# Queries of a local attention stage: two rotated products summed by accumulating transposes on TensorE or by an addition on GpSimd, with a newly planned order

## The chip, the cores and the metric

The kernel runs on one core of a Trainium2 chip. The time is the device time of one execution in microseconds (us). Three runs of the kernel before gave 1647.66, 1636.26 and 1648.2 us, with a median of 1647.66 us.

The engines are named as in the profile: PE is the matrix engine (PEld its weight loads), DVE the vector engine, ACT the scalar engine, POOL is GpSimd, SP only issues transfers.

## The reference, cut to what matters

The reference is a chain of eight blocks over 2048 tokens of 128 channels, each wrapped in a residual and a layer norm. The second block is a two-layer local attention network; it is where the change lies. Per layer, with 8 heads of 64 channels and sequences of 256 tokens:

```python
qkv = shift_token(x) @ wqkv
q, k, v = split into heads
q = l2norm(q) * qs
k = l2norm(k) * ksc
q = q * cos * scale + rotate_half(q) * sin * scale
k = k * cos / scale + rotate_half(k) * sin / scale
o = softmax(mask(8 * q @ k.T)) @ v      # a window of 64 and the window before it
x = x + o @ wo
x = x + gated_mlp(layernorm(shift_token(x)))
```

So every query is a sum of two products: the projected row times a table of cosines, and the half-swapped row times a table of sines. The third block is a Mamba network (a selective scan along the sequence). After them come a mixture of experts, two wide attention layers with their own feed-forward parts, another mixture of experts, and a last attention with a ternary linear layer.

## The kernel before, in words

The program is built in six stages: `rglru`, `local_mamba`, `moe1`, `chunked`, `moe2` and `typed`. Stage `local_mamba` holds the second and third blocks for 8 sequences of 256 tokens. Four sequences are in flight in the local network at a time, and behind them up to two Mamba sequences, so that the work of several generators is mixed (`interleave`, called at the end of `local_mamba`). In the profile the stage runs from about 47 us to about 800 us; the local attention part of it ends at about 627 us, and the last Mamba sequences go on alone.

One layer of one sequence is `local_block`. It calls `local_attention`, which calls `local_qk`, the function that is changed. `local_qk` works on tiles of 128 tokens by 512 channels (8 heads), two tiles for the queries (n = 0) and two for the keys (n = 1):

- PE projects a tile into a PSUM bank `qk` (two passes of 128x512 each in the profile, line 870, the shared `mm` helper);
- ACT squares it (L1085), DVE adds up the squares per head (L1086), giving the norms `ss`;
- DVE multiplies the PSUM tile by the cosine table into `t1` (L1090) and the half-swapped PSUM tile by the sine table into `t2` (L1092); the tables carry the learned scales;
- POOL clamps the norms (L1097), ACT takes their inverse root as exponential of a logarithm (L1098, L1099);
- POOL adds `t2` onto `t1` (L1105), for the keys it also multiplies by the inverse norm (L1107); the queries' inverse norm is applied later, in the softmax;
- PE transposes the sum in four 128x128 pieces into one PSUM bank `qkt` (L1110), and ACT copies the bank to the tile `q` or `k` (L1111).

Tiles `t1` and `t2` have three buffers each, the bank `qkt` has one, shared with the softmax's transposes (`pt`, L981). With 8 sequences, 2 layers and 2 tiles there are 32 query tiles and 32 key tiles, so 64 additions on L1105, of which half belong to the queries, and 256 transposes on L1110.

After `local_qk`: PE makes the scores `sc`, DVE takes their maximum (L1147), ACT the exponentials (L1153), POOL divides by the sums (L1158, a 128x1024 tile), PE transposes (L981) and multiplies by the values. The Mamba part's heaviest work is on DVE: for each of 8 groups of states a sequence has one product (L1304), one scan (L1306) and one product (L1307) on 128x1024 elements, all called `hs`.

The order of the instructions on each engine is not that of the program text. Class `_Order` takes all instructions with their dependences and runs a list scheduler over them (`plan`): an engine that comes free takes the ready instruction with the lowest rank, where the rank is the program's priority plus a hand-set offset from the table `BIAS` (one entry for each engine, tile name and stage), and changing the kind of work costs PE and ACT the offset `STAY`. Durations for this come from the table `LENGTHS` (time until the engine can issue the next, time until the result is there). `impose` then fixes that order for every engine, the transfer queues of SP, ACT and POOL among them. On the chip an engine works strictly in the imposed order, and waits when the next instruction's inputs are not there.

Of the kernel before, what the change touches and what calls it, by code (L numbers as in the profile page):

```python
# [311 lines left out]
class _Order:  # L312
# [14 lines left out]
    STAY = dict(PE=80, ACT=740)  # L327
    BIAS = {
        "ACT  1": 100, "ACT  5": 585, "ACT bt 3": 5, "ACT bt 5": -775, "ACT d 2": -425, "ACT da 2": -45, "ACT e 2": -5, "ACT e 4": 965, "ACT e 6": -20,
        "ACT got 3": 575, "ACT h 2": -200, "ACT ix 4": 15, "ACT k 2": 265, "ACT lavp 2": 210, "ACT lnrs 1": -10, "ACT lnrs 2": -160, "ACT lnsq 1": -135,  # L330
        "ACT lnsq 2": 15, "ACT ot 2": 10, "ACT ptsb 2": -595, "ACT ptsb 6": -515, "ACT q 2": 20, "ACT qsq 2": 10, "ACT r 2": -5, "ACT rg 1": 10,
        "ACT rg 2": -915, "ACT rn 2": 15, "ACT rs 4": 340, "ACT rs 6": -690, "ACT s 6": 200, "ACT sakq 2": -10, "ACT sg 3": -550, "ACT sh 5": -2525,
        "ACT spe 1": -220, "ACT spt 1": -50, "ACT st 6": 100, "ACT sz 2": 280, "ACT v 2": 885, "ACT vs 4": 320, "ACT xchunked 2": 15, "ACT xs 2": -610,
        "DVE biasfull 3": -335, "DVE biaspart 3": -20, "DVE bt 5": -5, "DVE c 1": 590, "DVE centre 0": 320, "DVE d 2": 10, "DVE decaypart 4": -600,
        "DVE e 4": 570, "DVE four 4": 100, "DVE fs 4": -70, "DVE gate 4": 340, "DVE get 2": 200, "DVE got 4": 530, "DVE identb 0": -50, "DVE k 6": 500,
        "DVE lg 2": 2240, "DVE lo 4": -265, "DVE mv 4": -660, "DVE mv 5": 100, "DVE mv 6": -485, "DVE nm 2": -3975, "DVE nm 6": 4960, "DVE nth 4": -45,
        "DVE oh 2": -725, "DVE oh 5": -10, "DVE ptsb 2": -3895, "DVE ptsb 6": 895, "DVE put 4": -395, "DVE put 5": 55, "DVE q 5": -825, "DVE q 6": -475,
        "DVE rc 2": -1225, "DVE rc 6": 10, "DVE route 2": -55, "DVE s 5": 10, "DVE sares 2": 70, "DVE sel 2": -1590, "DVE sg 3": -140, "DVE sm 4": 2720,
        "DVE spl 1": -215, "DVE ss 2": 370, "DVE st 4": 85, "DVE st 6": 1645, "DVE sum 4": 170, "DVE t 2": 440, "DVE u 2": 250, "DVE vs 4": 50,
        "DVE we 4": 1425, "DVE xc 2": 460, "DVE xla 4": -15, "DVE xlocal 2": -5, "DVE xmoe 5": -200, "DVE xmoe 6": -580, "DVE xpf 4": -370,  # L340
        "DVE xrglru 2": 120, "DVE xsa 4": 80, "DVE z 4": -1990, "PE a 2": -100, "PE acc 5": 155, "PE b 2": -35, "PE bt 3": 75, "PE bt 5": 50,
        "PE cum 2": -995, "PE cum 4": -25, "PE cum 5": -615, "PE fold 2": 2915, "PE g 2": -4155, "PE gate 2": 785, "PE kps 4": 135, "PE less 2": 295,
        "PE lg 2": 1680, "PE lg 4": 50, "PE ln 2": -10, "PE o 2": 10, "PE o 6": -10, "PE pg 5": 150, "PE ps 4": -15, "PE pt 4": -130, "PE pu 3": 220,
        "PE py 3": -200, "PE py 5": 170, "PE qk 2": 25, "PE qkt 2": -720, "PE raw 2": -8675, "PE rows 2": 400, "PE sc 2": -50, "PE sc 4": 65, "PE sc 6": 5,
        "PE v 5": 290, "PE vps 2": 4075, "PE vps 4": 25, "PE wo 2": 75, "PE wo 6": -85, "PE wout 2": -115, "PE xin 2": 1180, "PE xps 2": -2540, "PE y 2": 20,
        "PE z 2": -450, "PE zt 5": 560, "PE zt 6": 25, "POOL d 2": 130, "POOL e 6": -30, "POOL got 4": -200, "POOL h 2": 370, "POOL k 5": 400,
        "POOL k 6": 850, "POOL km 6": 1240, "POOL mean 0": 1510, "POOL places 5": -200, "POOL q 6": 20, "POOL rest 4": -65, "POOL rg 1": -800,
        "POOL rg 2": -200, "POOL rot 2": -400, "POOL s 6": -750, "POOL t 2": 550, "POOL zero 0": -655, "POOL zeros 1": 385, "SP bc 2": -970, "SP cst 3": 5,
        "SP got 3": 355, "SP got 5": 350, "SP rottable 0": 80, "SP rows 4": 210, "SP rowschunked 4": -105, "SP vec 0": -830, "SP w 0": 15, "SP w 3": 115,
        "SP wattn 2": 585, "SP wffn 2": 705, "SP wlocal 0": 1175, "SP wmoe 4": 520, "SP xs 2": -105, "SP ybuf 5": -200,  # L350
    }
    LENGTHS = {
        "ACT  LoadActFuncSet  ": (1178, 1283), "ACT d Ln 128x512 128x512": (535, 640), "ACT da Exp 128x255 128x255": (398, 503),
        "ACT e Abs 128x256 128x256": (460, 565), "ACT e Exp 128x128 128x128": (420, 525), "ACT e Exp 128x256 128x256": (461, 566),
        "ACT e Exp 128x512 128x512": (527, 632), "ACT four Exp 128x2 128x2": (100, 205), "ACT got DMACopy 128x512 128x512": (454, 3611),
        "ACT h TensorCopy 64x255 64x255": (295, 400), "ACT lnrs Exp 128x256 128x256": (315, 420), "ACT ot TensorCopy 128x512 128x512": (486, 591),
        "ACT qsq Square 128x512 128x512": (494, 599), "ACT r Relu 128x256 128x256": (460, 565), "ACT rg Exp 128x1020 128x1020": (1039, 1144),
        "ACT rg Exp 128x1024 128x1024": (998, 1103), "ACT rg Ln 128x1024 128x1024": (950, 1055), "ACT rn Exp 128x16 128x16": (110, 215),
        "ACT rn Ln 128x16 128x16": (112, 217), "ACT rs Exp 128x2 128x2": (96, 201), "ACT rs Ln 128x2 128x2": (98, 203),
        "ACT sh Silu 128x512 128x512": (492, 597), "ACT v TensorCopy 128x512 128x512": (485, 590), "ACT xc Identity 128x256 128x256": (460, 565),  # L360
        "ACT xc Silu 128x512 128x512": (526, 631), "ACT xchunked TensorCopy 128x256 128x256": (263, 368), "ACT xmoe Identity 128x256 128x256": (404, 509),
        "ACT xs TensorCopy 33x256 33x256": (257, 362), "ACT xsq Square 128x128 128x128": (297, 402), "DVE biaspart TensorCopy 96x256 96x256": (197, 282),
        "DVE decay TensorScalarPtr 128x512 128x512": (508, 593), "DVE decaypart TensorCopy 128x512 128x512": (331, 416),
        "DVE four TensorScalarPtr 128x4 128x4": (76, 160), "DVE ge TensorScalarPtr 128x256 128x256": (380, 465),
        "DVE ge TensorScalarPtr 85x256 85x256": (372, 457), "DVE got TensorScalarPtr 128x128 128x128": (258, 343),
        "DVE h TensorTensor 128x256 128x256": (312, 397), "DVE hs TensorScalarPtr 128x1024 128x1024": (2189, 2274),
        "DVE hs TensorTensor 128x1024 128x1024": (1116, 1201), "DVE mv BNStatsAggregate 128x2 128x6": (82, 167),
        "DVE nm TensorTensor 128x8 128x8": (66, 151), "DVE ptsb TensorCopy 128x512 128x512": (589, 674), "DVE rc Reciprocal 128x16 128x16": (160, 245),
        "DVE rc Reciprocal 128x4 128x4": (84, 169), "DVE rc Reciprocal 128x8 128x8": (106, 191), "DVE rg TensorScalarPtr 128x256 128x256": (577, 662),
        "DVE rg TensorTensor 128x1024 128x1024": (1109, 1194), "DVE rottable TensorScalarPtr 128x256 128x256": (261, 346),  # L370
        "DVE s TensorScalarPtr 128x128 128x128": (247, 332), "DVE s TensorTensor 128x256 128x256": (323, 408),
        "DVE sm TensorReduce 128x16 128x512": (593, 678), "DVE ss TensorReduce 128x8 128x512": (594, 679), "DVE st BNStats 128x6 128x128": (197, 282),
        "DVE sum TensorReduce 128x32 128x448": (810, 895), "DVE t TensorScalarPtr 128x256 128x256": (384, 469),
        "DVE t TensorTensor 128x512 128x512": (593, 678), "DVE vec TensorTensor 128x1 128x1": (59, 144), "DVE vec TensorTensor 85x1 85x1": (59, 144),
        "DVE vs TensorCopy 128x512 128x512": (594, 679), "DVE wlocal TensorScalarPtr 128x682 128x682": (481, 566),
        "DVE x TensorScalarPtr 128x256 128x256": (368, 453), "DVE xc TensorScalarPtr 128x254 128x254": (383, 468),
        "DVE xc TensorScalarPtr 128x255 128x255": (384, 469), "DVE xla TensorScalarPtr 128x256 128x256": (442, 527),
        "DVE xlocal TensorTensor 128x256 128x256": (311, 396), "DVE xpf TensorScalarPtr 128x256 128x256": (562, 647),
# [393 lines left out]
class _Kernel:  # L772
# [300 lines left out]
    def local_qk(self, l, h, w, rot, work, local, small, pools):  # L1073
# [6 lines left out]
        for n in range(2):  # L1080
# [20 lines left out]
            for t in range(2):  # L1101
# [4 lines left out]
                if n:  # L1106
                    nc.gpsimd.tensor_tensor(t1, t1, rn[:, 2 + t, :].unsqueeze(2).to_broadcast([P, 8, 64]), ALU.mult)  # L1107
                for c in range(4):
                    cols = slice(c * P, (c + 1) * P)
                    nc.tensor.transpose(ps[:, cols], f1[:, cols], self.ident)  # L1110
# [1300 lines left out]
```

## Time and profile before

| what | value |
|---|---|
| median of 3 runs | 1647.66 us (1636.26 to 1648.2) |
| profiled execution, its own time | 1644.68 us |
| its span | 1642.9 us |
| mean granted PE clock | 0.942 |
| busy share of the span: PE, DVE, ACT, POOL | 86%, 67%, 59%, 36% |
| L1105, additions of `t1` and `t2` on POOL | 64, median 1272 ns, 83.9 us in all |
| L1110, transposes of queries and keys on PE | 256, median 273 ns, 40.5 us in all |

The profile gives for each group of instructions how long they kept their engine busy, how long the engine stood idle just before them, and what ended that idle time. PE pipelines its work, so that instructions overlap and a matmul's duration is longer than the distance from its start to that of the next. The table by stretch (windows) sums the busy time of each engine between two times, counted from the start of the span.

### The profile page before, as it was taken

How to read it: one execution, taken by the hardware profiler on the slowest of the kernel's cores; microseconds unless marked ns; L12 is line 12 of the kernel's file. 1: busy time of each engine (PE TensorE's matmuls, PEld its weight loads, DVE VectorE, ACT ScalarE, POOL GpSimd, SP SyncE). 2: the span in 40 equal slices, each digit the busy share in tenths (PEclk: the TensorE clock that was granted, in tenths of full speed). 3: DMA queues.
4: the chain of work that ended last, by engine and by line, in shares of the span. 5: the costliest groups of instructions: out<-in, count | busy, mean ns of one | idle time of the engine just before them, and what ended most of it. 6: DMA issues, size and time to landing. Idle time of an engine off the chain costs nothing. (4 is left out here: it accounts for less than half of the span.)

```text
span 1642.9 us, 28581 instructions
## 1 busy us (share of the span) xinstructions
PE 1417.4 (86%) x10826; PEld 909.4 (55%) x10826; DVE 1102.3 (67%) x2182; ACT 968.6 (59%) x2656; POOL 587.5 (36%) x535
## 2 busy tenths in 40 slices
PE   2688998989898887777579999999998899899997
PEld 1354554545554544334366766777675576556664
DVE  5745568898989898698545557554546333279886
ACT  3777888787978869446125545455453222167775
POOL 1334544535462523101431222212212102467774
PEclk7789999989999999779789999999998899999998
DMA  5000012121212223155430000000000130000000
GB/s 199 1 1 1 1 40 65 40 60 45 65 40 65 53 52 91 52 179 189 151 119 1 8 12 11 10 5 8 32 18 24 46 121 26 26 9 8 5 8 11
DMA packets 45113, 77.97 MB, mean 47 GB/s; under 512 B 5580, under 2 KB 21988, under 8 KB 43824
## 3 DMA queue, kind: packets, MB, share of 16 engines
q1 hardware_dynamic: 39648, 70.02, 14.0%
q0 software_dynamic: 3216, 5.07, 1.1%
q8 instruction: 85, 1.39, 0.4%
q10 hardware_dynamic: 2112, 1.05, 0.2%
q14 instruction: 52, 0.43, 0.1%
HBM read 66.87 MB, written 10.76 MB: 47 GB/s over the span
## 5 line engine op out<-in xcount | busy, mean ns | idle before, releaser
L870 PE MATMUL y<-hs,ident 128*128 128x512 f32 x256 | 139.7, 659 | 35.9 <-DVE hs L1307 35.6
L1158 POOL TENSOR_TENSOR e<-e,rc 128x1024 f32<-128x1024 f32 x32 | 78.0, 2437 | 202.7 <-DVE rc L1157 194.3
L1306 DVE TENSOR_TENSOR_SCAN hs<-da,hs 128x1024 f32<-128x1024 f32 x64 | 149.1, 2331 | 0.2
L2259 ACT ACTIVATE e<-sc,nm 128x128 f32<-128x128 f32 (+1 forms) x256 | 105.2, 427 | 46.6 <-DVE nm L2254 40.3
L1153 ACT ACTIVATE e<-sc,nm,rn 128x128 f32<-128x128 f32 x256 | 114.3, 466 | 13.8 <-DVE nm L1148 13.5
L981 PE MATMUL pt<-ident,e 128*128 128x128 f32 x768 | 114.2, 278 | 9.4 <-POOL e L1158 4.9
L1302 ACT ACTIVATE da<-d,na 128x255 f32<-128x255 f32 x256 | 109.3, 504 | 17.5 <-DVE hs L1306 13.7
L1836 POOL TENSOR_TENSOR e<-e,rc 128x512 f32<-128x512 f32 x32 | 34.0, 1064 | 219.8 <-DVE rc L1835 154.2
L981 PEld LDWEIGHTS pt<-ident,e 128*128 128x128 f32 x768 | 88.5, 141 | 42.5 <-issue 16.1
L2262 POOL TENSOR_TENSOR e<-e,rc 128x1024 f32<-128x1024 f32 x48 | 90.8, 1896 | 39.1 <-DVE rc L2261 32.1
L1105 POOL TENSOR_TENSOR t<-t,t 128x512 f32<-128x512 f32 x64 | 83.9, 1316 | 58.0 <-DVE t L1092 51.6
L1811 ACT COPY kp<-kps 128x512 f32<-128x512 f32 x128 | 74.7, 583 | 49.0 <-PE kps L870 46.4
L1658 POOL DMA_INDIRECT got<-ybuf,get x48 | 45.7, 952 | 159.2 <-DMA ybuf<-ys 97.1
L870 PEld LDWEIGHTS y<-hs,ident 128*128 128x128 f32 x256 | 48.5, 205 | 82.5 <-DVE hs L1307 54.2
L1304 DVE TENSOR_TENSOR hs<-u,bc 128x1024 f32<-128x1024 f32 x64 | 84.3, 1328 | 2.9 <-POOL u L1291 2.9
L1307 DVE TENSOR_TENSOR hs<-hs,bc 128x1024 f32<-128x1024 f32 x64 | 80.6, 1260 | 0.0
L1847 ACT COPY vs<-vps 128x512 f32<-128x512 f32 x64 | 37.4, 585 | 67.1 <-PE vps L870 53.6
L983 DVE COPY ptsb<-pt 128x512 f32<-128x512 f32 x104 | 68.8, 675 | 11.6 <-PE pt L981 9.3
L870 PE MATMUL qk<-w_local,h 128*128 128x512 f32 x128 | 69.3, 631 | 7.5 <-DVE t L1092 7.1
L870 PE MATMUL vps<-sa_vp,x_lf 128*32 128x512 f32 x512 | 68.4, 594 | 0.0
L1847 DVE COPY vs<-vps 128x512 f32<-128x512 f32 x64 | 43.3, 682 | 37.2 <-PE vps L870 25.1
L2057 DVE TENSOR_TENSOR sh<-sh,pu 128x512 f32<-128x512 f32 x32 | 22.0, 688 | 67.1 <-PE pu L870 54.0
(380 smaller groups left out, 3782.4 us busy)
## 6 DMA issues: line engine op xcount, KB each, us to landing
bc<-xs SPq DMA_DIRECT2D x128, 256.0 KB
w_moe<-in_e_dram SPq DMA_DIRECT2D x16, 768.0 KB
w_attn<-in_w_dram SPq DMA_DIRECT2D x4, 1024.0 KB
w_local<-in_w_dram SPq DMA_DIRECT2D x2, 1557.0 KB
places<-zeros SPq DMA_DIRECT2D x2, 1280.0 KB
got<-places SPq DMA_DIRECT2D x6, 256.0 KB
ybuf<-ys SPq DMA_DIRECT2D x8, 160.0 KB
x_in<-in_x_dram SPq DMA_DIRECT2D x1, 1024.0 KB
```

Of the source, the lines that this page charges most:

```text
L870: return self.nc.tensor.matmul(out, lhsT, rhs, start=start, stop=stop)
L981: self.last = self.nc.tensor.transpose(pt[:, j * P : (j + 1) * P], src[:, j * P : (j + 1) * P], self.ident)
L1105: nc.gpsimd.tensor_add(t1, t1, t2)
L1153: nc.scalar.activation(e[:, j, g, :], scs[:, j, g, :], AF.Exp, bias=nm[:, j, g : g + 1], scale=rq[:, j, g : g + 1], accum_out=sm[:, j, g : ...
L1158: nc.gpsimd.tensor_tensor(e, e, rc.unsqueeze(3).to_broadcast([P, 2, 4, P]), ALU.mult)
L1302: nc.scalar.activation(da[:, n, c, 1:S], d[:, c, 1:S], AF.Exp, scale=na[:, i : i + 1])
L1304: nc.vector.tensor_tensor(hs, u.unsqueeze(1).to_broadcast(shp), bn, ALU.mult)
L1306: nc.vector.tensor_tensor_scan(line(hs), line(da), line(hs), 0.0, ALU.mult, ALU.add)
L1307: nc.vector.tensor_tensor(hs, hs, cn, ALU.mult)
L1847: i = copy(v[:, c, :, :].rearrange("p a b -> p (a b)"), ps)
L2259: nc.scalar.activation(e[:, i, :], sc[:, i, :], AF.Exp, bias=nm[:, i : i + 1], accum_out=sm[:, i : i + 1])
L2262: nc.gpsimd.tensor_tensor(e, e, rc.unsqueeze(2).to_broadcast([P, n, keys]), ALU.mult)
```

## The change

For the queries, POOL no longer adds `t2` onto `t1`. Both go to PE as they are: each 128x128 piece of `t1` is transposed into the bank, and the same piece of `t2` is transposed onto it with accumulation in PSUM. The keys still get their sum and their inverse norm from POOL and one transpose a piece. The transposes are now written as matmuls with the transpose flag, so that the first one of a bank starts the accumulation and the last one stops it. POOL so has 32 additions fewer (32 instead of 64 on that line), and PE has 128 transposes more (384 instead of 256).

```diff
                 ps = self.psum("B", "qkt")
-                nc.gpsimd.tensor_add(t1, t1, t2)
+                parts = [f1] if n else [f1, t2.rearrange("p h d -> p (h d)")]
                 if n:
+                    nc.gpsimd.tensor_add(t1, t1, t2)
                     nc.gpsimd.tensor_tensor(t1, t1, rn[:, 2 + t, :].unsqueeze(2).to_broadcast([P, 8, 64]), ALU.mult)
                 for c in range(4):
                     cols = slice(c * P, (c + 1) * P)
-                    nc.tensor.transpose(ps[:, cols], f1[:, cols], self.ident)
+                    for i, part in enumerate(parts):
+                        nc.tensor.matmul(
+                            ps[:, cols], part[:, cols], self.ident, start=c == 0 and i == 0, stop=c == 3 and i == len(parts) - 1, is_transpose=True
+                        )
```

The planner's tables are all new. `STAY` goes from 80 to 90 for PE and from 740 to 620 for ACT. `BIAS` has 186 entries in place of 175, of which 124 names are in both; a few of them, from both sides:

```
name        before   after
DVE t 2        440    1435
PE qkt 2      -720     -50
PE raw 2     -8675    -315
DVE nm 2     -3975   -1730
POOL t 2       550    1180
DVE nm 6      4960      95
```

`LENGTHS` gets other durations, mostly within a few per cent of the old ones (a 128x128 transpose into `qkt` 116 in place of 117 ns to the next issue). So the imposed order of every engine and every queue can differ in all six stages, not only around the queries.

## The prediction

> **What bounds the kernel now.** I read the page's strips first, to see which engine is full where.
>
> ```profile
> PE   2688998989898887777579999999998899899997
> DVE  5745568898989898698545557554546333279886
> POOL 1334544535462523101431222212212102467774
> PEclk7789999989999999779789999999998899999998
> ```
>
> A slice is 41 us. The local attention lies in slices 2 to 15: there PE is eight or nine tenths busy, DVE too from the sixth slice, POOL about four. The table by stretch gives sums; I chose the cuts by the start of the Mamba scans (240 us), the last query tile (627 us) and the end of the stage (812 us).
>
> ```profile
> core 0: us, PE busy (x) PEld busy (x) DVE busy (x) ACT busy (x) POOL busy (x), PEclk, DMA share, GB/s
> 47.00:240.00 193.00, 160.82 (x1034) 96.27 (x1033) 117.21 (x191) 148.51 (x398) 80.70 (x88) 0.92 0.01 3
> 240.00:440.00 200.00, 175.40 (x991) 104.75 (x991) 178.16 (x215) 164.89 (x437) 98.10 (x83) 0.96 0.20 58
> 440.00:627.00 187.00, 165.32 (x980) 98.17 (x978) 164.98 (x213) 149.72 (x385) 83.66 (x70) 0.99 0.22 55
> 627.00:812.00 185.00, 122.10 (x530) 66.69 (x531) 144.41 (x171) 96.03 (x218) 41.60 (x30) 0.83 0.42 140
> 900.00:1270.00 370.00, 357.10 (x4090) 253.40 (x4082) 210.35 (x703) 178.97 (x436) 78.92 (x86) 0.99 0.04 13
> ```
>
> From 240 to 627 us (387 us) PE works 340.7 and DVE 343.1: each idles some 45 us, and neither alone sets the pace. From 47 to 240 PE idles 32 us, DVE 76. From 627 to 812 DVE leads, with the last scans. The wide attention (900 to 1270) is PE's, 97% busy. POOL, which the change relieves, is never the fullest here.
>
> Then the groups of the tile `t`, whose waits say what the removed addition cost:
>
> ```profile
> L1110 PE MATMUL qkt<-ident,t x256: 270/273/421, 51.8 to 626.2; 128*128 128x128 f32 x128
> L1105 POOL TENSOR_TENSOR t<-t,t x64: 1259/1272/2293, 49.4 to 620.8; 128x512 f32<-128x512 f32 x64
> its engine sat idle before it (us, times) until:
>   DVE t L1092: 51.6, 34
> ...
>   PEld qkt L1110: 9.8, 20
> ```
>
> POOL waited for DVE's second product in 34 of 64 cases: it was there early, so the additions mostly start when `t2` is done. PE's weight queue waited 9.8 us in 20 cases for a tile `t` from POOL; by the waits of the stage 7.0 of it are for L1105, the sums of queries and keys together. So the sums' 83.9 us are nearly all hidden, behind other sequences' work on PE.
>
> **The change, part by part.** I sum against the profiled execution: 1644.68 us, of which 1642.9 are its span and 1.8 lie around it. It stands 2.98 us under the median of the runs (1647.66).
>
> *128 more transposes on PE* (32 query tiles by 4 pieces). A duration of 273 ns overlaps with the next; what counts is the distance of starts:
>
> ```profile
> 182.48 1.02 PE L870 MATMUL qk<-w_local,h 128*128 128x512 f32 x2
> 183.34 0.63 PE L1110 MATMUL qkt<-ident,t 128*128 128x128 f32 x4
> 183.81 0.60 PE L870 MATMUL ln<-ln_sq,mean 128*128 128x256 f32 x2
> ```
>
> Four pieces occupy PE for 183.81 - 183.34 = 0.47 us, and 32 tiles by 0.47 make 15.0 us. No row shows an accumulating transpose; the plain one is the nearest, so I take its price. Lower end 0: between 47 and 627 us PE stands idle 193 + 387 - 501.5 = 78.5 us, and all 15 may fall there. Upper end 15.0. Of these two I take half, 7.5, because from 240 to 627 us PE and DVE are equally full, so a longer PE queue is felt about half the time.
>
> *A rule weighed against this row.* The Trainium skill, "TensorE: Matmul & The Clock Gate", Part 4, gives about 275 ns for a 128x128 transpose in one kernel, most of it access latency, which speaks against the change. The trace has nearly that duration, a median of 273 ns, but four starts in 0.47 us; by the page's figure the term would be 128 x 0.275 = 35 us (an estimate from that page), where the starts make it 15.0.
>
> *32 additions fewer on POOL.* 32 x 1.27 = 40.7 us leave POOL. Their own path is worth little: the keys' sums come later in every block, with the inverse norm behind them, so the block's scores wait for keys. I book 0; the ends are -7.0 (all of PE's waits for L1105 gone) and, since PE now waits for DVE's `t2` itself, something above nothing, priced under the first rival. Behind PE's waiting transpose then stands everything of the other three sequences, PE being in order, and ACT's copy of `q`.
>
> *Collisions of POOL and DVE.* At 414.10 us POOL begins a sum of 1.27 us, and DVE shows:
>
> ```profile
> 414.41 3.38 DVE L1304 TENSOR_TENSOR hs<-u,bc 128x1024 f32<-128x1024 f32 x2
> 417.71 2.28 DVE L1306 TENSOR_TENSOR_SCAN hs<-da,hs 128x1024 f32<-128x1024 f32 x1
> ```
>
> Two products take 3.38 us where two medians make 2.43: 0.95 us lost. Over the kernel, the means of L1304, L1306 and L1307 (1328, 2331, 1260 ns) lie 115, 51 and 45 ns over their medians (1213, 2280, 1215), times 64: 13.5 us, the most that could come back (end -13.5; other end 0). POOL is busy 181.8 us from 240 to 627, its sums 46.1 of that, the queries' half 23.1 or 13%. Thirteen per cent of 13.5 is 1.8; I take -2.
>
> *A rule on the same row.* The Trainium skill, "SBUF — State Buffer", on who interferes with whom, says that a DVE instruction with two SBUF inputs and a GpSimd instruction that reads SBUF exclude each other for the whole instruction. Were every query sum between 240 and 627 us (18 of them) to block DVE for its length, the gain would be 23 us (an estimate by that page); the trace's excess over all POOL work is only 13.5.
>
> *Tiles and queues.* `t2` is held until PE has read it instead of POOL; both have three buffers and DVE waited 1.9 us for `qkt` before its products, so nothing is booked, with the cover being those buffers; gone, it costs up to those 1.9 us again. ACT's copies and all transfers stay in number: 0.
>
> *The new order.* Every queue is ordered anew, SP's and POOL's too, in all stages. Nothing in the trace prices an order that hasn't run. It can gain what idle time the pacing engines have and lose as much; the two rivals below put -28 and +24 on it. In the middle I take 0.
>
> Sum: 7.5 - 2 + 0 = +5.5, so 1650.2 us beside the profiled 1644.68, and 1653.2 beside the median. I predict 1653 us.
>
> **The rivals.** *PE paces and waits for the second product* (slower). For: PE is 83% to 88% busy, and 34 of 64 sums began at the end of `t2`, so PE placed as tightly would stand there. The nearest row is PE's `qk` waiting for DVE's `t`, between 47 and 240 us: 7.1 us in 6 times, 1.2 us each. If half of the 32 tiles are met that way, 16 x 1.2 = 19, and the 15.0 is felt whole: +34 at most; with 10 such waits 15 + 12 = +27, or 1675 us. It decides from two waits on (15 + 2.4 = 17.4, above 1%). Against: the planner can put other sequences' matmuls between, as it does now.
>
> *The order loses elsewhere* (slower). The last attention (1394 to 1643 us) has PE 226.4 of 249 busy, the wide one 357.1 of 370: they hold 23 and 13 us of PE's idle time, hardly anything to win and as much again to lose. A loss of two thirds of 36 is +24: 1672 us. It decides from 17 us.
>
> *The scans move forward* (faster). DVE idles 44 us from 240 to 627, while 24 of the 64 scan groups run after 627 (the rows of `hs` in that stretch), in the stretch where DVE leads. A group is 1.21 + 2.28 + 1.22 = 4.7 us; each that an order with freer POOL fits into the idle time shortens the tail by so much. Six make -28: 1620 us. It decides from four (18.8 us). For: POOL makes the Mamba inputs (L1287 to L1291) in the queue with the sums. Against: the scans' inputs come from the local part, which PE's longer queue delays.
>
> **How the numbers follow.** A measurement of this kernel can't tell less than about 1% (16.5 us) from no change. Chances: the sum 0.45, with a range of its own of 1638 to 1664 (-7.0 and -2 below the median; 1% above it, which takes in the +15); PE waits 0.20 (1675); order elsewhere 0.13 (1672); scans forward 0.22 (1620). So faster 0.22, same 0.45, slower 0.33. The range reaches to the centre of the faster case, 1620, and above to 1682, the sum of +34 on the median: some 0.11 is left out below and 0.05 above.
>
> **What would show it.** L1105 has 32 entries, the transposes 384, and four more of them push the next matmul 0.47 us further. Right: PE busy from the start of the stage to the last query is some 15 us more, the stretch longer by 5 to 10, DVE's `hs` means closer to their medians. The first rival: PE rows `qkt` waiting for DVE L1092 with 10 us or more. The second: the stretches after 900 us longer. The third: fewer than 20 scan groups after the last query. What would make me wrong above all is an order that is better or worse by over 1%, for which the trace has no row.

## The result, and the profile after

| | before | changed |
|---|---|---|
| median of the runs | 1647.61 us (4 runs) | 1663.23 us (4 runs, 1660.4 to 1665.23) |
| profiled execution, its span | 1644.68, 1642.9 us | 1662.56, 1660.8 us |
| mean granted PE clock | 0.942 | 0.948 |

The ratio of the runs is 1.0121, with a 95% interval of 1.0085 to 1.0158; the two medians differ by 15.6 us, 0.95%. The changed kernel is slower by about 1%, in the profiled executions at a PE clock that was no lower. The predicted 1653 us lies 10 us under its median.

The page's sums and strips of the changed kernel; a slice is 41.5 us:

```profile
PE 1438.6 (87%) x10954; PEld 911.7 (55%) x10954; DVE 1103.0 (66%) x2182; ACT 976.8 (59%) x2662; POOL 535.1 (32%) x503
PE   3589998989898887767579999999997998999997
DVE  5855579897979798588455556654556233378885
POOL 1124343524252414101431122211312103466674
PEclk7799999999999999788789999999998999999998
```

PE has 128 entries more, as it must, and 21 us more busy time; POOL has 52 us less. ACT has six entries more: six more loads of its function tables (75 for 69, by the order of its instructions, 1.28 us each in the trace). The changed code has none of its own, so they come from the new order.

The table by stretch, cut at the changed kernel's own start of the scans, last query, end of the local stage, first experts, wide attention, shared experts, and last attention:

```profile
core 0: us, PE busy (x) PEld busy (x) DVE busy (x) ACT busy (x) POOL busy (x), PEclk, DMA share, GB/s
45.70:233.00 187.30, 154.54 (x1066) 95.77 (x1066) 114.07 (x184) 143.74 (x391) 58.73 (x70) 0.95 0.00 1
233.00:445.00 212.00, 188.41 (x1114) 111.48 (x1112) 188.86 (x229) 181.65 (x473) 85.93 (x77) 0.97 0.22 60
445.00:632.00 187.00, 165.41 (x950) 96.58 (x950) 157.98 (x204) 146.22 (x363) 67.46 (x62) 0.98 0.20 55
632.00:820.70 188.70, 125.78 (x533) 67.17 (x531) 143.71 (x171) 96.33 (x218) 39.89 (x29) 0.82 0.42 135
...
908.60:1280.40 371.80, 359.18 (x4077) 250.95 (x4069) 212.55 (x703) 177.88 (x436) 78.67 (x86) 0.99 0.04 12
...
1408.10:1660.80 252.70, 234.60 (x1886) 139.70 (x1886) 175.89 (x422) 144.49 (x622) 153.99 (x106) 0.98 0.03 10
```

Up to the last query PE works 154.5 + 188.4 + 165.4 = 508.4 us, where before had 501.5. The same events in both traces, in us:

| stretch | before | changed |
|---|---|---|
| first `qk` product to last transpose of queries and keys | 580.9 | 588.1 |
| from there to the last scan's product `y` | 166.3 | 167.6 |
| to the first experts, then to the wide attention | 20.8, 85.3 | 22.0, 88.0 |
| wide attention | 371.3 | 371.8 |
| shared experts up to the last one's product | 167.7 | 164.2 |
| last shared product to the end: the last attention | 205.3 | 216.1 |

So 7 us are lost where the change is, and 10.8 in the last attention, whose program is the same. The groups of PE there, before and then changed:

```profile
L870 PE MATMUL sc<-km,q 64*128 64x512 f32 x192 | 54.0, 640 | 0.8 <-DVE mv L949 0.8
L981 PE MATMUL pt<-ident,e 128*128 128x128 f32 x384 | 52.0, 275 | 1.4 <-POOL e L2262 1.3
```

```profile
L870 PE MATMUL sc<-km,q 64*128 64x512 f32 x192 | 60.7, 640 | 1.0 <-DVE mv L949 1.0
L981 PE MATMUL pt<-ident,e 128*128 128x128 f32 x384 | 56.0, 279 | 1.1 <-POOL e L2266 0.9
```

The columns are busy time, mean duration of one, and idle time before them. The same 192 entries of the same 640 ns keep PE busy 6.7 us longer, and the idle time before them has hardly grown: the instructions overlap less than they did. That is what the later experiments are about.

The tile `qkt` in the changed kernel, with what its users waited for:

```profile
L1112 PE MATMUL qkt<-ident,t x384: 270/273/421, 46.4 to 631.1; 128*128 128x128 f32 x192
its engine sat idle before it (us, times) until:
  ACT q L1115: 13.2, 14
...
  DVE t L1090: 6.0, 7
...
  DVE t L1092: 1.8, 4
```

The wait for `t2` (L1092), which the first rival feared, is 1.8 us in all, and 7.8 us together with the waits for `t1` (L1090).

### The profile page after: what moved, and what is told of

It is laid out like the page before. It is cut to its first block, busy times and chain, and to the rows that moved or that the text cites. A ratio compares the mean times of both kernels' runs of the same rounds, so it can differ in the third digit from the quotient of the medians.

```text
span 1660.8 us, 28779 instructions
## 1 busy us (share of the span) xinstructions
PE 1438.6 (87%) x10954; PEld 911.7 (55%) x10954; DVE 1103.0 (66%) x2182; ACT 976.8 (59%) x2662; POOL 535.1 (32%) x503
## 3 DMA queue, kind: packets, MB, share of 16 engines
q10 hardware_dynamic: 2112, 1.05, 0.2%
## 4 chain that ended last, share of the span: by engine, by line
PE 54%; ACT 17%; DVE 16%; issue 6%; POOL 4%; DMA 2%; another core or an unknown queue 0%; ACTq 0%; SPq 0%; DVEq 0%; POOLq 0%
PE vps L870 7%; PE sc L870 7%; PE kps L870 6%; ACT e L1157 5%; PE out L870 4%; PE pt L981 4%; PE pu L870 3%; PE pg L870 3%; ACT da L1306 3%; PE o L870 2%; DVE hs L1310 2%; DVE hs L1308 2%; PE py L870 2%; DVE hs L1311 2%; PE hps L870 2%
## 5 line engine op out<-in xcount | busy, mean ns | idle before, releaser
L1157 ACT ACTIVATE e<-sc,nm,rn 128x128 f32<-128x128 f32 x256 | 114.6, 467 | 13.1 <-DVE nm L1152 10.5
L981 PE MATMUL pt<-ident,e 128*128 128x128 f32 x768 | 117.6, 279 | 4.4 <-ACT ptsb L983 1.7
L2258 DVE TENSOR_REDUCE nm<-sc 128x4 f32<-128x1024 f32 (+1 forms) x48 | 58.5, 1218 | 19.8 <-PE sc L870 19.5
L983 ACT COPY ptsb<-pt 128x512 f32<-128x512 f32 x88 | 51.4, 584 | 26.8 <-PE pt L981 19.4
L870 PE MATMUL sc<-msk,identb 128*128 128x512 bf16 (+2 forms) x224 | 49.4, 357 | 19.0 <-ACT e L1157 18.8
```

The costliest lines, as they stand in the source:

```text
L870: return self.nc.tensor.matmul(out, lhsT, rhs, start=start, stop=stop)
L981: self.last = self.nc.tensor.transpose(pt[:, j * P : (j + 1) * P], src[:, j * P : (j + 1) * P], self.ident)
L983: copy(sb.rearrange("p a b -> p (a b)"), pt)
L1157: nc.scalar.activation(e[:, j, g, :], scs[:, j, g, :], AF.Exp, bias=nm[:, j, g : g + 1], scale=rq[:, j, g : g + 1], accum_out=sm[:, j, g : ...
```

## The experiments

My theory at this point: the changed code costs some 5 to 8 us, half of PE's 15, and the other 10 are the new order in the later stages. Against it stood that all of it comes from the changed code, or none.

The table holds all runs; each ratio is against the kernel before on the same chip. They ran on three chips, four kernels on each, and before took 1629.7, 1628.9 and 1645.2 us there, so whole times are compared by ratio only.

| kernel | ratio to before, 95% interval |
|---|---|
| the change in the order of before | 1.0006 (0.9987 to 1.0025) |
| transposes doubled, sums kept | 1.0060 (1.0039 to 1.0080) |
| sums cut | 0.9997 (0.9983 to 1.0010) |
| transposes doubled, sums cut | 1.0010 (0.9998 to 1.0022) |
| changed kernel, order of before from the first experts on | 1.0047 (1.0029 to 1.0064) |
| before, order of the changed kernel from the first experts on | 1.0063 (1.0046 to 1.0080) |
| changed kernel, outputs ahead of the next scores | 1.0179 (1.0162 to 1.0196) |
| the change in the order of before, outputs ahead | 1.0050 (1.0031 to 1.0069) |
| changed kernel, parted halves joined | 1.0106 (1.0091 to 1.0121) |
| before, 13 units' halves parted | 1.0085 (1.0068 to 1.0102) |
| changed code, planner's tables of before | 1.0130 (1.0112 to 1.0148) |
| code of before, planner's tables of the changed kernel | 1.0186 (1.0162 to 1.0209) |

**The change without the new order.** The planner is shown the program of before, with a small POOL instruction priced like the sum in the sum's place; the transposes of `t2` are put into PE's planned sequence right behind those of `t1`.

```diff
-                nc.gpsimd.tensor_add(t1, t1, t2)
+                if n:
+                    nc.gpsimd.tensor_add(t1, t1, t2)
+                else:
+                    small = nc.gpsimd.tensor_tensor(self.side, t2[:, 0, 0:8], t2[:, 0, 0:8], ALU.add)
+                    self.as_long.add(small.ins.name)
...
-                    nc.tensor.transpose(ps[:, cols], f1[:, cols], self.ident)
+                    i = nc.tensor.matmul(ps[:, cols], f1[:, cols], self.ident, start=c == 0 or n > 0, stop=n > 0, is_transpose=True)
+                    if not n:
...
+                        j = nc.tensor.matmul(ps[:, cols], t2.rearrange("p h d -> p (h d)")[:, cols], self.ident, start=False, stop=c == 3, is_transpose=True)
+                        self.behind[i.ins.name] = j.ins
```

> The change made in the order of before: every engine keeps its sequence, the 128 transposes of t2 stand right behind those of t1 and add to the same bank, and where POOL's 32 sums of the queries stood it adds 128x8 elements instead. Theory 1 (the change itself costs about half of PE's 15 us, the other 10 us of the 15.6 us are the new order after 900 us): 5 to 8 us over before, ratio 1.003 to 1.005, and all stretches after 900 us as long as before's to within 2 us. Theory 2 (all of it comes from the changed code, the later stages only inherit it): 13 to 16 us over before, ratio 1.008 to 1.010. Theory 3 (the 15 us of PE are covered, all of it is the order): within 2 us of before.

Measured 1.0006: by this ratio theory 3. The change itself costs 1 us, -2 to +4, in an order that was never made for it, and theory 2's 13 to 16 us fall. My own 5 to 8 us are not refuted, for two other readings of the same runs give about 5. In the trace the local stretch is 585.7 us, 4.8 over before's 580.9: PE is busy 10.0 us longer there (512.4 for 502.4) and idle 5.2 us less. And the runs of one kernel differ by the clock that PE was granted. On this chip 24 of the 28 runs of before had a clock of 0.938 to 0.943, with a median of 1630.0 us, and 4 had 0.945 to 0.949, with 1622.0. Of the 12 runs with the change 5 had 0.941 to 0.943, with 1635.3, and 7 had 0.945 to 0.949, with 1626.8. By these medians the change costs 5 us at like clock; more of its runs had the higher clock, and that hides it in the ratio. Whether the change itself brings the higher clock, no run shows. So its direct cost is 1 to 5 us.

**PE's term and POOL's term, each by itself and both together**, in the same order. First only the doubled transposes:

```diff
-                    nc.tensor.transpose(ps[:, cols], f1[:, cols], self.ident)
+                    i = nc.tensor.transpose(ps[:, cols], f1[:, cols], self.ident)
+                    if not n:
...
+                        j = nc.tensor.transpose(ps[:, cols], f1[:, cols], self.ident)
+                        self.behind[i.ins.name] = j.ins
```

> Before with its order, and only PE's cost added: each of the queries' 128 transposes is made twice into the same place, POOL's sums stay, the output is the same. It measures the term of PE alone. Theory 1: 7 to 9 us over before, that is half of 128 x 0.117 us = 15.0 us. If PE sets the pace wherever the transposes stand: 15 us, ratio 1.009. If they lie in PE's idle time: 0 to 2 us.

Then only the cut sums:

```diff
-                nc.gpsimd.tensor_add(t1, t1, t2)
+                if n:
+                    nc.gpsimd.tensor_add(t1, t1, t2)
+                else:
+                    small = nc.gpsimd.tensor_add(t1[:, 0, 0:8], t1[:, 0, 0:8], t2[:, 0, 0:8])
```

> Before with its order, and only POOL's relief: the 32 sums of the queries are cut from 128x512 to 128x8 elements, so that most of the sine product is left out of the queries; PE keeps its 256 transposes. It measures what 40.7 us less of POOL are worth in the same order. Theory 1 as booked: 0 for the path and 2 us at most from fewer collisions with DVE, so 0 to 2 us under before. Rival (POOL's sums were the last thing that the queries' transposes waited for): 7 us under before, ratio 0.996.

The transposes alone cost 0.60% of 1629.7 = 9.8 us (6.4 to 13.0), nearer two thirds of 15.0 than half. The cut sums alone bring 0.5 us (-1.6 to 2.8), that is, nothing clear of noise. If the two were independent, the change would have to cost 9 us. It costs 1. So both diffs at once:

> Before with its order, the queries' 128 transposes made twice and POOL's 32 sums of the queries cut to 128x8 elements at once, so that most of the sine product is left out of the queries. The first run of the doubled transposes alone gave 1.006, the cut sums alone 0.9997, and the change itself in this order 1.0006. Theory A (the sums stand in the path of the transposes, so that what PE takes longer is given back when POOL is relieved): 1.000 to 1.002, as the change itself. Theory B (the two terms are independent and add up): 1.0057, 9 us over before; then the accumulating transposes must be cheaper than a repeated one.

Measured 1.0010, inside theory A's numbers. By the ratios doubled transposes cost 9.8 us beside the sums and 2.1 us beside cut sums, and the intervals of 1.0060 and 1.0010 do not meet. But what theory A says of the path, that the transposes waited for the sums, is not what the traces show. The local stretch with doubled transposes, first with the sums and then with cut sums:

```profile
46.60:638.20 591.60, 518.88 (x3127) 316.09 (x3127) 461.06 (x630) 463.61 (x1217) 261.80 (x239) 0.95 0.14 38
46.80:633.90 587.10, 510.94 (x3128) 312.43 (x3127) 460.21 (x630) 464.25 (x1218) 228.35 (x239) 0.96 0.14 38
```

Beside 580.9 us of before and 580.7 with the sums cut alone, the doubled transposes cost 10.7 and 6.4 us in the traces. The 4.5 us between the two rows are not waits: for the same work in the same order PE is busy 7.9 us less, at a granted clock of 0.96 for 0.95, and idle 3.4 us more. The runs agree: with the sums all 6 had a clock of 0.939 to 0.943, with cut sums all 12 had 0.943 to 0.949, so they can't be compared at like clock. POOL's relief by itself is worth nothing; beside the longer transposes it went with a higher clock and 4.5 to 8 us, and whether it brings that clock the runs do not show.

**The new order, cut in two at the first experts.** The planner takes its three tables by stage:

```diff
-        self.rank = [x.bass_priority + self.BIAS.get(f"{k} {g}", 0) for k, g, (x, _, _) in zip(self.key, stage, self.ops)]
+        self.rank = [x.bass_priority + (self.LATE_BIAS if g >= 3 else self.BIAS).get(f"{k} {g}", 0) for k, g, (x, _, _) in zip(self.key, stage, self.ops)]
```

and `STAY` and `LENGTHS` in the same way. In the first kernel the code and the early tables are the changed ones and the late ones those of before; in the second the code and the early tables are those of before and the late ones the changed.

> The changed kernel, its order up to the end of the local stage and the second product's start as it is, and the planner's costs and due times of before for everything from the first experts on, so that from there each engine's sequence is that of before. Theory 1 (10 us of the loss are the new order after the first experts begin): 1653, 9 to 11 us under the changed kernel, ratio to before 1.003 to 1.005. Theory 2 (the later stages only inherit a late start): as the changed kernel, 1663, ratio 1.009 or more.

> The kernel before, code and order untouched up to the start of the second product, and from the first experts on the planner's costs and due times of the changed kernel, whose program is the same there. Theory 1 (the later stages lose by their new order alone): 10 to 14 us over before, ratio 1.006 to 1.009, with 10 to 11 us of it between the last shared expert's product and the end. Theory 2 (they lose only because what comes before them is late): within 2 us of before.

Measured 1.0047 and 1.0063. The order of the late stages costs 0.63%, 10 us, in a kernel that has nothing else of the change: theory 1, against inheritance. The stretch of the last attention is 215.8 us there and 205.3 in the other. By the ratios the early order costs 1.0047 - 1.0006 = 0.41%, 7 us; in the traces it is 2.0 us, a local stretch of 587.7 for the 585.7 of the change in the order of before. At a clock of 0.943 or less the medians are 1636.9 us (8 runs) and 1635.3 (5 runs). So how the 7 us of the local stretch divide between the code and the early order stays open: 1 and 7 by the ratios, 5 and 2 by the traces. The parts 0.06 + 0.41 + 0.63 = 1.10% stand beside the 1.21% measured for the whole.

One wait of the early order is plain in PE's timeline of the changed kernel, with the idle time and its releaser at the end of the line; the last line is DVE's, from the same time:

```profile
67.17 0.94 PE L870 MATMUL sc<-k,q 64*128 64x128 f32 x12
78.75 1.01 PE L870 MATMUL sc<-msk,identb 128*128 128x512 bf16 x2 [10.64 <-ACT e L1157]
66.16 6.54 DVE L1035 RECIPROCAL rg<-rg 128x1024 f32<-128x1024 f32 x1
```

PE stands still for 10.64 us in one piece; the longest such wait of the stage before was 4.29. ACT made its exponentials for these scores in a block only from 75.07 us on, after waiting 6.03 us for DVE's `nm`, and DVE stood until 72.70 in one reciprocal of the first block, which stands ahead of `nm` in its sequence. What this wait costs the whole was not tried by itself.

**Why the last attention takes 10.8 us longer: the number of shape changes?** In the trace PE changes its tile shape (rows by columns of the array) 206 times there and not 180. In the order of before an output group (128x32) stands directly ahead of scores (64x128) 20 times, in the changed one never. I moved all outputs there, in PE's planned sequence, with all other sequences kept.

```diff
         order, _ = self.plan()
+        order["PE"] = self.turned(order["PE"])
...
+            if kind(i) == "PE o":
+                if len(held) == 8:
+                    out, held = out + held, []
+                held.append(i)
+                continue
+            if held and (kind(i) in ("PE wo", "PE sc") or len(held) < 8):
+                out, held = out + held, []
+            out.append(i)
```

> The changed kernel with PE's order in the last attention altered in one way: each unit's 16 output products (128x32 tiles) stand directly ahead of the next unit's scores (64x128 tiles) instead of directly behind its own, so that PE changes its tile shape 159 times in this stage and not 206 times (before: 180). Theory S (the 10.8 us that the last attention lost are the 26 changes of shape more, 0.42 us each): the stretch from the last shared expert's product to the end falls by 15 to 20 us from 216.1, the ratio to before to 1.000 to 1.004. Rival (the loss is waits for DVE and ACT that the new order moved): no change of that stretch beyond 3 us, or a longer one, since the outputs are later now.

> The change in the order of before, as in the run of 1.0006, with the same alteration in the last attention: 160 changes of PE's tile shape there and not 180. Theory S: 20 x 0.42 = 8 us less, ratio 0.995 to 0.997, faster than both kernels. Rival: 1.000 to 1.002 as without it, or worse by the waits for outputs that now come one group later.

Both slower. The stretch grew from 216.1 to 228.7 and from 205.4 to 213.5 us. The table by stretch for the last attention of the second kernel, without and then with the alteration:

```profile
1425.50:1630.90 205.40, 188.97 (x1722) 114.85 (x1720) 164.24 (x403) 135.61 (x608) 135.30 (x88) 0.97 0.03 8
```

```profile
1420.20:1633.70 213.50, 189.22 (x1722) 114.73 (x1720) 164.28 (x403) 136.06 (x608) 135.29 (x88) 0.98 0.02 8
```

With 20 changes of shape fewer PE is busy as long as before (189.2 for 189.0) and idle 7.9 us longer, more of it now for POOL's division and DVE's norms (L2300: 5.5 us for 1.3, L984: 6.6 for 4.5). In the changed kernel, 47 changes fewer took 3.6 us from its busy time (198.0 to 194.4) and added 16.2 to its idle time. Theory S, 0.42 us each, falls.

**Or the company that the matmuls have.** A score of the last attention is two matmuls, one on PE's rows 0 to 63 and one on rows 64 to 127; each is two entries in the trace. PE's timeline of before shows a unit with its halves side by side, that of the changed kernel one with a projection between:

```profile
1497.85 1.13 PE L870 MATMUL sc<-km,q 64*128 64x512 f32 x4
1498.81 0.38 PE L870 MATMUL sc<-decay,onesb 64*128 64x512 bf16 x2
```

```profile
1507.23 1.12 PE L870 MATMUL sc<-km,q 64*128 64x512 f32 x2
1508.28 1.13 PE L870 MATMUL proj<-x_moe,w 128*128 128x256 f32 x4
1509.34 0.69 PE L870 MATMUL sc<-km,q 64*128 64x512 f32 x1
1509.35 0.39 PE L870 MATMUL sc<-decay,onesb 64*128 64x512 bf16 x1
1509.87 0.59 PE L870 MATMUL sc<-km,q 64*128 64x512 f32 x1
```

Side by side, both halves take 1498.81 - 1497.85 = 0.96 us; one half alone takes 1508.28 - 1507.23 = 1.05. The halves run at the same time when nothing stands between. The Trainium skill, "TensorE: Matmul & The Clock Gate", Part 3, says that tiles in different row groups run concurrently; the runs agree, with a pair as long as a single half. To see what this is worth, the parted halves of the changed kernel were joined, and halves in the kernel before were parted:

```diff
...
+                if j > k + 1 and half(ring[j]) and open_:
+                    ring.insert(k + 1, ring.pop(j))
...
```

```diff
...
+            if half(ring[k]) and half(ring[k + 1]) and side(ring[k + 2]):
+                ring.insert(k + 1, ring.pop(k + 2))
...
```

> The changed kernel with one alteration in the last attention: in 6 of its 48 units the two halves of a score (64x128 tiles that lie in different halves of PE's rows) are parted by other matmuls of 128 rows; here the second half is put directly behind the first. PE's changes of tile shape stay 206. Theory F (halves that stand side by side run at the same time: whole units take 0.98 us in the trace, parted ones 1.60 us): the stretch from the last shared expert's product to the end falls by 3.7 to 6.4 us, from 216.1 to 210 to 212. Theory S (the number of shape changes sets it): no change, 216 to within 1 us.

> The kernel before, code and order kept, but in 13 of the 48 units of the last attention the matmul of 128 rows that stood behind the two halves of the score is put between them. Theory F: 13 x 0.62 us = 8 us over before, ratio 1.004 to 1.006, all of it between the last shared expert's product and the end (205.3 to 212 to 214). Rival (PE runs the halves one after the other in any case, and what was seen is another wait): within 2 us of before.

PE's group of these matmuls, joined and then parted, to be read beside 60.7 of the changed kernel and 54.0 of before:

```profile
L889 PE MATMUL sc<-km,q 64*128 64x512 f32 x192 | 54.0, 640 | 1.0 <-DVE mv L968 1.0
```

```profile
L882 PE MATMUL sc<-km,q 64*128 64x512 f32 x192 | 68.5, 640 | 0.8 <-DVE mv L961 0.8
```

Both ways theory F holds. Joined, the busy time of these matmuls is back at before's 54.0 and the stretch falls by 3.8 us to 212.3, with the shape changes still 206. Parted in 13 units, the stretch grows by 13.1 us to 218.4, 1.0 us a unit where I expected 0.6, and the whole by 0.85%. Parting them also takes the changes of shape from 180 to 206; at 3.6 us for 47 changes, as above, 26 of them make some 2 of the 13.1 us (an estimate). The joining has no such second term. So 3.8 of the 10.8 us are parted halves. The joined kernel's whole ratio, 1.0106, is not told apart from the changed kernel's 1.0121. The other 7 us are not settled: the transposes `pt` stay at 56.0 us against 52.0 even when the halves are joined, and in the changed order other matmuls are put between them more often (the 384 stand in 75 groups there and in 58 before), but no run undid that.

**Code and tables by themselves.** Changed code with all three tables of before, and the reverse; the first lines of the two edits, the first beside the changed kernel and the second beside the kernel before:

```diff
-    STAY = dict(PE=90, ACT=620)
+    STAY = dict(PE=80, ACT=740)
```

```diff
-    STAY = dict(PE=80, ACT=740)
+    STAY = dict(PE=90, ACT=620)
```

and `BIAS` and `LENGTHS` whole in the same way.

> The changed code, planned anew with the planner's costs and due times of before. From the second product on every engine's sequence is that of before. Theory 1 (the changed code in an order that was made for it costs about 1 us, and a new order of the local stage takes what it takes by its own waits): the last attention at 205.3 us and the whole at 1.002 to 1.006 of before, its loss all ahead of the first experts. Rival (the new costs and due times are needed to make the change pay): slower than the changed kernel, over 1.012.

> The code of before, planned anew with the costs and due times of the changed kernel. Theory 1 (the order costs about 7 us ahead of the first experts and 10 to 12 us from there on, the changed code next to nothing): 1.009 to 1.012 of before, as the changed kernel itself, with the last attention at 216 us. Rival (the new order is good for the changed code and only bad without it): over 1.015. Rival (the changed code is what costs): under 1.005.

Measured 1.0130 and 1.0186, both against my theory's numbers. The second goes with its first rival, over 1.015; the first, with an interval from 1.0112, is not told apart from the changed kernel's 1.0121. The code planned with the old tables has its last attention at 205.2 us, as expected, but its local stretch takes 604.0 us, where the same code in the order of before took 585.7: planning anew around a program that has changed a little cost 18 us here (two traces from two chips). The new tables bring this stretch to 588.1 and lose 10.8 us in the last attention. With the code of before they make the local stretch 595.9 and the last attention 216.0. So what the tables gain in the local stretch does not carry over from one program to the other, what they lose in the last attention does, and the small cost of the change itself shows only in an unchanged order. None of the twelve was faster than before by more than the noise.

## Why the prediction was off, point by point

The time lay in the range, 10 us over the forecast. It is at the edge of the likeliest case (within 1%, up to 1664 us): 0.95% over before by the medians, 1.2% by the ratio. That it came so near is in part the width of that case. What the sum priced measured 1 to 5 us, and most of the rest came from the term that it held at nothing.

- *128 more transposes, 7.5 of 15.0 us.* The price holds: in 24 places of the changed kernel's trace eight of them stand in a row, and the next matmul starts 0.87 to 1.04 us after the first, 0.93 at the median, 0.116 each. Beside the sums, in the order of before, they cost 9.8 us by the ratio. The 275 ns of the Trainium skill ("TensorE: Matmul & The Clock Gate", Part 4), which I weighed against the row, would have made 35 (an estimate from that page); the measurement decides for the row. PE's busy time up to the last query rose by 6.8 us and not by 15, in an order that also changed other things.
- *Sums off POOL, booked at 0.* Right alone (0.5 us). Beside the longer transposes the kernel with cut sums was 8 us faster by the ratios and 4.5 in the traces, but as PE's busy time at a higher clock and not as waits; I had no term for the clock. The direct effect of both edits was +1 by the ratio and +5 at like clock and in the trace, beside my +5.5.
- *Collisions, -2.* The means of `hs` after are these:

```profile
L1310 DVE TENSOR_TENSOR_SCAN hs<-da,hs 128x1024 f32<-128x1024 f32 x64 | 147.6, 2307 | 0.9 <-ACT da L1306 0.7
L1308 DVE TENSOR_TENSOR hs<-u,bc 128x1024 f32<-128x1024 f32 x64 | 87.1, 1373 | 4.1 <-POOL u L1295 2.6 <-PE y L870 0.9 <-DMA bc<-xs 0.6
L1311 DVE TENSOR_TENSOR hs<-hs,bc 128x1024 f32<-128x1024 f32 x64 | 78.5, 1230 | 0.0
```

  They lie 157, 26 and 15 ns over the medians (1216, 2281, 1215), times 64: 12.7 us, where before had 13.5. The 0.8 is less than the 2 that I took. My share of 13% spread the loss evenly over POOL's work, and it is not even: 4.6 of the 13.5 us are one product, beside two sums and two multiplications. Before:

```profile
333.11 5.81 DVE L1304 TENSOR_TENSOR hs<-u,bc 128x1024 f32<-128x1024 f32 x1
333.34 2.49 POOL L1105 TENSOR_TENSOR t<-t,t 128x512 f32<-128x512 f32 x2
335.79 2.04 POOL L1107 TENSOR_TENSOR t<-t,rn 128x512 f32<-128x512 f32 x2
```

  In the changed kernel, where POOL's sums are those of the keys alone, the same meeting is there at 249.51 us, again with 5.81.
- *The new order, "in the middle I take 0".* This is the step that failed: it measured 10 us late and 2 to 7 early. That nothing in the trace prices an order is true, but the middle of an unpriced replacement was not zero here: the four runs that replaced an order, in whole or in part, all lie over before, by 0.5% to 1.9%. Why the kernel before had the better order, they do not show.
- *First rival, PE waits for `t2`.* Refuted: 1.8 us in 4 times, not 10 or more.
- *Second rival, the order loses elsewhere.* It came in part, at the place that I named: the last attention. I priced it as idle time to lose (two thirds of 36 us, together with the wide attention); it came as busy time, 9 us of it, PE's 188.9 growing to 198.0 for the same instructions. The wide attention lost nothing (371.8 for 371.3).
- *Third rival, scans forward.* Refuted: 24 groups still run after the last query, as before:

```profile
L1310 DVE TENSOR_TENSOR_SCAN hs<-da,hs x24: 2240/2282/2292, 636.4 to 793.7; 128x1024 f32<-128x1024 f32 x24
```

## What to carry to other kernels

Separate the edit from the order that comes with it: hold every engine's sequence fixed and put the edit in, before asking what the edit is worth. Run two edits singly and together, and before a difference of a few us is called a wait, compare runs at like granted clock and see in the trace whether busy or idle time moved. And when a stage loses time in which its program is the same, compare the busy time of equal groups first: the same entries at the same duration with more busy time have lost their overlap.

## What the runs showed of the hardware that I had not expected

- Two 64-row matmuls on different halves of PE's rows take 0.96 us together and 1.05 us for one alone. One matmul of 128 rows between them cost 1.0 us for each of 13 units, of which two changes of tile shape are a small part.
- A transposition that accumulates onto another has the price of a plain one: eight in 0.93 us, where four plain ones took 0.47.
- One DVE product of 128x1024 that overlapped four POOL instructions of 128x512 lasted 5.81 us, where the median is 1.21: it ended 1.1 us after the last of them, in both traces.
- Changes of PE's tile shape were cheap in this stage: 20 fewer left the busy time as it was, 47 fewer took 3.6 us from it.
- The same instructions in the same order take different times on different chips: the wide attention 371.2 us in the trace of the parted halves and 363.3 in that of the cut sums, both at a granted clock of 0.99, and the shared experts 167.9 and 157.3, at 0.93 and 0.97. What makes the difference the runs do not show.
- One kernel's runs on one chip differ by their granted clock: 1622.0 us at 0.945 to 0.949 and 1630.0 at 0.938 to 0.943, for the kernel before.
